# Step groups, statistics and normalisation in an attention and depthwise-convolution kernel

## The chip, the cores and the metric

The kernel runs on one core of a Trainium2 chip, in float32 throughout. The core has a TensorE for matrix products (PE in the profile, with its weight loads as PEld), a VectorE (DVE), a ScalarE (ACT), a GpSimd (POOL) and a SyncE (SP); each works through its own queue in order, and they wait for each other by semaphores. Transfers run on 16 DMA engines; the kernel issues them from SP, from POOL and, at the end, a few from ACT. The metric is the device time of one launch in microseconds (us), as the median of several runs.

## The reference

The input is 16 images of 384 channels and 32 x 32 points. Two residual layers, each behind a group norm over 32 groups of 12 channels:

```
x = x + proj(attention(gn(x)))      # 8 heads of 48, 1024 tokens, softmax over tokens
x = x + dwconv7x7(gn(x), w_sym)     # w_sym: mean of the four rotations of the weight
```

with `gn(v) = (v - mean) / sqrt(var + 1e-5)` per image and group, `attention` from `w_qkv` (3 x 384 rows) with a scale of 48^-0.5, and `proj` with a bias.

## The kernel before, in words

**Layout.** An image is three tiles of 128 channels by 1024 points. The heads are worked in four pairs, called units (u, four an image, 64 in all); the two heads of a pair lie at partitions 0 and 64, so that two products run at once.

**Attention.** A step n is one block of 128 keys against one half of the queries, for a pair: 16 steps a unit, 64 an image, 1024 in all. `s_step` (L331, L339) makes the scores of a step on PE (two products over 48 rows each, into a PSUM tile of two banks) and takes their exponential on ACT into a tile e. `av_step` (L347) multiplies e with v, whose extra column of ones yields the softmax's sum; eight steps accumulate in one PSUM bank, and `take` (L358) copies it out on ACT. The scores' PSUM pool `ps_s` has three buffers, which qk, v, the projection and the convolution on PE use too; `ps_o`, for the sums of AV, has two. The steps go in groups of GS = 4: four S steps, then four AV steps. No maximum is subtracted; the sums are tested at the end (`check_vector`), and a second, general version of the program would run if one were out of range. It doesn't here.

**Around it.** Per image: `qk_step` six times (L280; PSUM copied out on ACT), `v_step` four times (L306, L315), `qk_rest`, which moves the rows of the fourth pair by DMA; after a unit `sums_out`, `invert` and `divide` (through HBM: sums out, reciprocal on DVE, and back broadcast, then a product on DVE, L383); after four units `proj_step` three times (L398), whose ACT copy adds the bias (L406) and whose POOL DMA adds x (L407). The last image ends in a shorter way: `divide_at_once` (L418, L420, L421) sums by a product with a mask and divides at once, `proj_part` (L431) projects with unpacked weights in four parts, and `residual` (L440) adds on DVE.

**Statistics.** `Stats.channels` (L195) takes channel statistics on DVE; `gather` sends them through HBM to one row per group (ch, gs: L201, L203); `groups` (L208 to L220) makes 1/sigma on POOL by a power and sends scale and bias back through HBM (gr, sc). For the first x and the last x1, `groups_on_pe` (L236) does it with small products instead. `apply` normalises: x on ACT (L265), x1 on POOL (L261, three tiles an image) except in the last image.

**Convolution.** For each tile 49 taps on DVE (L455): `scalar_tensor_tensor` adds a shifted, weighted xn to the sum, in place. Up to three tiles are worked in turns, so that neighbouring taps don't depend on each other. Four tiles (two of each of the last two images) are done on PE instead (`conv_on_pe`, L557, 16 pieces, after the attention of the last image), and their result is added on DVE (L570).

**Order.** The order in each queue is written out by a plan while the program is made. It keeps two clocks, `clock` for PE and `vclock` for DVE, advanced by fixed prices (`US_STEP` 1.716 a step, `US_TURN` 0.353 a group, `US_QK` 5.3, `US_V` 4.0, `US_PROJ` 5.3, a tap by its area). `after(wait, cost, f)` puts work for DVE (and the DMAs behind it) on a heap, due `wait` later; `catch_up` issues due work or, if there is none, taps, until `vclock` reaches `clock`. The qk and v work of the next image, `chunks`, is issued between groups as a credit grows. The plan fixes only the order; the true times come from the engines' waits.

Of the kernel before, what the change touches and what calls it, by code (L numbers as in the profile page):

```python
# [16 lines left out]
P = 128  # L17
# [27 lines left out]
def kernel(  # L45
# [64 lines left out]
    def run(general):  # L110
        tag = "g" if general else "f"
        with ExitStack() as stack:
# [11 lines left out]
            epool = pool("epool", 6)  # L124
# [13 lines left out]
            PE_K = [NK - 1, NK - 2]  # L138
            PE_TILES = [(b, k) for b in (B - 2, B - 1) for k in PE_K]

# [24 lines left out]
            nc.sync.dma_start(wp, w_proj_t.rearrange("(k p) c -> p k c", p=P))  # L165
# [7 lines left out]
            vs = []  # L173
            for i in range(2):
                t = wpool.tile([P, NT, VW], F32, name=f"v_{i}")
                nc.gpsimd.memset(t, 1.0)
                vs.append(t)
# [4 lines left out]
            mhalf = wpool.tile([P, NK], F32, name="mhalf")  # L182
            nc.gpsimd.memset(mhalf, -0.5)

# [3 lines left out]
            class Stats:  # L188
# [16 lines left out]
                def groups(self):  # L205

                    mv = small.tile([GROUPS, 2], F32, tag="mv", name=f"mv_{self.name}")
                    nc.vector.bn_aggr(mv, self.gs)  # L208
                    ve = small.tile([GROUPS, 1], F32, tag="ve", name=f"ve_{self.name}")
                    nc.gpsimd.tensor_scalar(ve, mv[:, 1:2], EPS, None, ALU.add)  # L210
                    af = small.tile([GROUPS, 2], F32, tag="af", name=f"af_{self.name}")
                    nc.gpsimd.tensor_tensor(af[:, 0:1], ve, mhalf[0:GROUPS, 0:1], ALU.pow)
                    nc.gpsimd.tensor_tensor(af[:, 1:2], mv[:, 0:1], af[:, 0:1], ALU.mult)
                    nc.gpsimd.tensor_scalar(af[:, 1:2], af[:, 1:2], -1.0, None, ALU.mult)
                    gr_d = ddram.tile([GROUPS, PER, 2], F32, tag="gr", name=f"gr_{self.name}")
                    nc.gpsimd.dma_start(
                        gr_d, af.unsqueeze(1).to_broadcast([GROUPS, PER, 2])
                    )
                    self.sc = small.tile([P, NK, 2], F32, tag="sc", name=f"sc_{self.name}")
                    nc.gpsimd.dma_start(  # L220
                        self.sc, gr_d.rearrange("g e s -> (g e) s").rearrange("(k p) s -> p k s", p=P)
                    )

                def groups_on_pe(self, masks):
# [29 lines left out]
                    nc.gpsimd.tensor_tensor(self.sc[:, :, 0], d, mhalf, ALU.pow)  # L254
# [4 lines left out]
                def apply(self, dst, src, k, engine=None):  # L259
                    if engine is not None:  # L260
                        engine.tensor_scalar(  # L261
                            dst, src, self.sc[:, k, 0:1], self.sc[:, k, 1:2], ALU.mult, ALU.add
                        )
                        return
                    nc.scalar.activation(  # L265
                        dst,
                        src,
                        AF.Identity,
                        bias=self.sc[:, k, 1:2],
                        scale=self.sc[:, k, 0:1],  # L270
                    )

# [28 lines left out]
            def v_step(b, t2):  # L301
# [11 lines left out]
                for j in range(2):  # L313
                    dst = vs[b % 2][:, 2 * t2 + j, 0 : HEADS * (D + 1)]
                    nc.scalar.copy(  # L315
                        dst.rearrange("p (h d) -> p h d", d=D + 1)[:, :, 0:D],
                        ps[:, j, 0:C].rearrange("p (h d) -> p h d", d=D),
                    )

            def v_of(u, i, j):  # L320
                b, p = divmod(u, NP)
                c = (2 * p + j) * (D + 1)
                return vs[b % 2][:, i, c : c + 64]
# [90 lines left out]

            def divide_at_once(u, h):
# [6 lines left out]

            late, pps = {}, {}
# [28 lines left out]
            def conv_tap(b, k, dy, dx):  # L452
                (oy, iy), (ox, ix) = region(dy, dx)
                acc = x1s[b, k].rearrange("p (h w) -> p h w", w=W)[:, oy, ox]
# [199 lines left out]
            clock, vclock = 0.0, 0.0  # L654
# [3 lines left out]
            GS = 4  # L658
            PER_B = 2 * NT * NP

            def now():
                return max(clock, vclock)
# [7 lines left out]
            def us_tap(dy, dx):  # L670
                late_us = 0.06 if active[0][0] >= B - 2 else 0.0
                return ((H - abs(dy)) * (W - abs(dx)) + (130 if len(active) > 1 else 270)) / 940 + late_us

            def tap():
# [3 lines left out]
                if not active:  # L678
                    return 0.0
                b, k, n = active[0]  # L680
                took = us_tap(*TAPS[n])
# [8 lines left out]

            def catch_up(to):
                nonlocal vclock
                while vclock < to:
# [6 lines left out]
                    if took:  # L700
                        vclock += took
                    else:
                        vclock = min([to] + [t[0] for t in later[:1]])

# [21 lines left out]

            def project(b):
# [6 lines left out]
            def x1_part(b, k):  # L734
# [4 lines left out]
                if k == NK - 1:  # L739
                    st.gather()  # L740
                    after(7.0, 0.8, lambda: x1_groups(b, st))

            def x1_groups(b, st):
                st.groups()
                after(9.0, 0.0, lambda: x1_chains(b, st))

            def x1_chains(b, st):
                on_pe = [t for t in PE_TILES if t[0] == b]
                for k in range(NK - 1, -1, -1):
                    tail = b == B - 1  # L750
                    conv_begin(st, b, k, (nc.gpsimd, None, nc.vector)[k] if tail else nc.gpsimd)
# [9 lines left out]
            def begin_x(b):  # L761
                load_x(b)
                after(10.0, 3.8, lambda: x_channels(b))

            def x_channels(b):
# [4 lines left out]
                after(12.0, 0.8, lambda: x_groups(b, st))  # L770

            def x_groups(b, st):
                st.groups()
                after(35.0, 0.0, lambda: x_apply(b, st))

            def x_apply(b, st):
                for k in range(NK):
                    st.apply(xns[b][:, k, :], xns[b][:, k, :], k)
                ready[b] = now() + 6.0

            def finish(u):
                sums_out(u)
                if u < U - 1:
                    after(7.0, 0.3, lambda: finish2(u))
# [5 lines left out]
            def finish3(u):  # L790
                b, p = divmod(u, NP)
                divide(u)
                if p == NP - 1:
                    proj.append((now() + 4.0, b))

            def queue(b):
                chunks.extend(("qk", b, i) for i in range(4))
                chunks.extend(("v", b, i) for i in range(2))
                chunks.extend(("qk", b, i) for i in range(4, 6))
                chunks.extend(("v", b, i) for i in range(2, 4))  # L800
# [5 lines left out]
            st.groups_on_pe(masks_0.rearrange("p (b c) -> p b c", c=P))  # L806
# [5 lines left out]
            while chunks:  # L812
                issue(chunks.popleft())
            vclock = clock
# [41 lines left out]

            credit = 0.0
            for n0 in range(0, NS, GS):
                b, r = divmod(n0, PER_B)
# [5 lines left out]
                for n in range(n0, n0 + GS):  # L865
                    s_step(n)
                if n0 == NS - 2 * GS:
                    after(3.5, 4.2, lambda: None)
                    divide_at_once(U - 1, 0)
                if n0 == NS - GS:  # L870
                    for o in range(NK):
                        proj_part(B - 1, o, (0, 1))
                    clock += 2 * US_PROJ
                for n in range(n0, n0 + GS):
                    av_step(n)
                    u, h, i = n // (2 * NT), n // NT % 2, n % NT
                    if i == NT - 1:
                        take(u, h)
                        if h == 1:
                            finish(u)  # L880
                clock += GS * US_STEP + US_TURN

                credit = min(credit + 12.0 * GS / PER_B, 2.0)
                if proj and proj[0][0] <= clock:
                    project(proj.popleft()[1])
                elif credit >= 2:
                    while chunks and credit >= 1:
                        kind, cb, i = chunks[0]
                        first = {"qk": 2 * NT * (i // 2), "v": 0, "rest": 2 * NT * 3}[kind]
                        if ready.get(cb, 1e9) > clock or r + GS < first:  # L890
                            break
                        issue(chunks.popleft())
                        credit -= 1
                catch_up(clock)
                if b == 1 and r == 0:
                    conv_prepare()
                if b == B - 1:

                    if r == 4 * GS:
# [3 lines left out]
                    if r == 8 * GS:  # L903
                        w4 = w_proj_4.rearrange("(t p) c -> p t c", p=P)
                        nc.sync.dma_start(wp, w4[:, 0:NK])
                        nc.sync.dma_start(late["w3"], w4[:, NK])
                    if r == 6 * GS:
                        conv_matrices(1, flat2(qkpool.tile([P, 2, N], F32, tag="qk", name="mat_1")))
                    if r == 8 * GS:
# [3 lines left out]
                    if r >= 9 * GS and (b, 0) not in x1s and all(c[0] > b - 2 for c in active):  # L913
# [5 lines left out]
                    if r in (10 * GS, 12 * GS, 14 * GS):  # L919
                        loads(1)  # L920


            late["tail"] = True
            b = B - 1
            divide_at_once(U - 1, 1)
            for t in (NP - 2, NP - 1):
                for o in range(NK):
                    proj_part(b, o, (t,))
            clock += US_PROJ * 4 / 3 + 1.0
            st = Stats(f"x1_{b}")  # L930
            for o in range(NK):
                residual(b, o)
                st.channels(x1s[b, o], o)
            conv_piece()
            st.groups_on_pe(late["masks"])
            clock += 7.0
            x1_chains(b, st)
# [58 lines left out]
```

## Time and profile before

| | us |
|---|---|
| median of 3 runs | 3023.71 (3022.39 to 3024.68) |
| the profiled execution, its whole time | 3021.88 |
| its span, first to last instruction | 3020.0 |
| mean granted TensorE clock | 0.994 of full |

Busy time by stage, from the windows of the trace (us busy in the window):

| window | PE | DVE | ACT | POOL |
|---|---|---|---|---|
| 0 to 40 | 22.60 | 8.20 | 4.55 | 9.79 |
| 40 to 260 (first image's attention) | 220.00 | 14.36 | 95.47 | 20.69 |
| 300 to 1000 | 697.78 | 641.51 | 317.19 | 119.57 |
| 1000 to 2000 | 1000.00 | 982.17 | 460.19 | 300.76 |
| 2000 to 2700 | 699.81 | 687.97 | 321.42 | 205.49 |
| 2870 to 2920 (last projection) | 34.64 | 38.28 | 1.83 | 2.76 |
| 2970 to 3020 (end) | 35.48 | 38.46 | 0.00 | 2.13 |

How to read the lines that follow. A line of the chain or of a timeline has its start, its length, the engine, what it does (output <- inputs) and how many instructions it merges; brackets at its end hold the idle time before it and what ended that. A line of a group has the busy time in all and the mean of one in ns, then idle time before it. Matmul ends are modelled, and records of one float32 product come in two.

### The profile page before, as it was taken

To read this page: it belongs to the slowest core of one execution; us is meant where nothing else is said; L and a number is where in the kernel's file an instruction comes from. 1 tells how busy PE (TensorE), PEld (TensorE's weight loads), DVE (VectorE), ACT (ScalarE), POOL (GpSimd) and SP (SyncE) were. 2 spreads that over 40 slices of the span, in tenths; PEclk is the share of its full clock that TensorE was granted. 3 is DMA by queue.
4 is the path that set the end of the run, shared out by engine and by line. 5 is a ranking of instruction groups with operands and counts; after the bars stand their busy time and mean duration, and the time that the engine had idled before them with its cause. 6 is when DMAs were issued, how large, how long until landed. Compare 5 with 4: busy or idle time off the path is not lost.

```text
span 3020.0 us, 30559 instructions
## 1 busy us (share of the span) xinstructions
PE 2970.3 (98%) x11658; PEld 1166.2 (39%) x11658; DVE 2616.1 (87%) x2553; ACT 1298.7 (43%) x1469; POOL 728.3 (24%) x426
## 2 busy tenths in 40 slices
PE   7999999999999999999999999999999999999978
PEld 4333343433334343343434334343433434333333
DVE  1101898997999999999999999999999999999788
ACT  1534535354453545435353453535445353544400
POOL 1021004020140604215060320505133060411500
PEclk9999999999999999999999999999999999999989
DMA  2113031121312112131211313122131312212234
GB/s 70 38 23 67 15 66 37 39 53 33 67 36 58 23 52 51 36 70 39 52 30 36 66 36 66 42 46 37 36 66 36 66 37 51 37 43 38 89 83 114
DMA packets 68332, 149.42 MB, mean 49 GB/s; under 512 B 30880, under 2 KB 33168, under 8 KB 66640
## 3 DMA queue, kind: packets, MB, share of 16 engines
q1 hardware_dynamic: 47536, 90.80, 12.2%
q0 software_dynamic: 18560, 52.31, 7.8%
q10 hardware_dynamic: 2080, 4.26, 0.6%
q8 instruction: 94, 1.54, 0.2%
q14 instruction: 62, 0.51, 0.1%
HBM read 99.35 MB, written 29.49 MB: 43 GB/s over the span
## 4 chain that ended last, share of the span: by engine, by line
PE 90%; DVE 5%; issue 3%; POOL 1%; DMA 1%; ACT 0%; POOLq 0%; SPq 0%; DVEq 0%
PE ps_s L331 29%; PE acc L347 29%; PE ps_qk L280 16%; PE ps_v L306 8%; PE ps_proj L398 8%; DVE x L455 4%; POOL ve_x L210 1%; DMA wc<-in_w_conv 0%; PE ps_st_x L236 0%; DVE bs_x L195 0%; DMA out<-x 0%; DVE x L570 0%; DMA sums<-sum 0%; DMA sum<-o 0%; DVE o L383 0%
## 5 line engine op out<-in xcount | busy, mean ns | idle before, releaser
L455 DVE SCALAR_TENSOR_TENSOR x<-xn,wsym,x 128x960 f32<-128x960 f32 (+9 forms) x2156 | 2379.2, 1175 | 19.5 <-POOL xn L261 17.6
L339 ACT ACTIVATE e<-ps_s 128x1024 f32<-128x1024 f32 x1024 | 967.0, 1030 | 395.0 <-PE ps_s L331 390.1
L331 PE MATMUL ps_s<-qk 48*128 48x512 f32 x4096 | 948.6, 602 | 2.2 <-ACT e L339 2.2
L347 PE MATMUL acc<-e,v 128*64 128x512 f32 x4096 | 935.4, 598 | 0.0
L331 PEld LDWEIGHTS ps_s<-qk 48*128 48x128 f32 x4096 | 373.1, 186 | 566.8 <-issue 430.6
L347 PEld LDWEIGHTS acc<-e,v 128*64 128x64 f32 x4096 | 271.5, 136 | 632.4 <-issue 561.0
L280 PE MATMUL ps_qk<-x,wqk 128*128 128x512 f32 x1152 | 506.8, 596 | 2.3 <-DVE x L261 2.3
L407 POOL DMA_DIRECT2D x<-in_x x45 | 39.6, 881 | 1414.8 <-ACT x L406 1414.8
L280 PEld LDWEIGHTS ps_qk<-x,wqk 128*128 128x128 f32 x1152 | 217.0, 190 | 284.9 <-issue 278.3
L210 POOL TENSOR_SCALAR ve_x<-mv_x 32x1 f32<-32x1 f32 x30 | 313.8, 10461 | 44.4 <-DVE mv_x L208 43.3
L287 ACT COPY qk<-ps_qk 128x1024 f32<-128x1024 f32 x96 | 97.2, 1012 | 463.4 <-PE ps_qk L280 463.4
L306 PE MATMUL ps_v<-wv,x 128*128 128x384 f32 x768 | 254.5, 488 | 0.0
L398 PE MATMUL ps_proj<-o,wp 128*128 128x512 f32 x540 | 235.7, 595 | 0.2 <-DVE bs_x L195 0.2
L358 ACT COPY o<-acc 128x512 f32<-128x512 f32 x128 | 75.1, 587 | 307.2 <-PE acc L347 307.2
L261 POOL TENSOR_SCALAR xn<-x,sc_x 128x1024 f32<-128x1024 f32 x46 | 198.0, 4309 | 33.5 <-DMA sc_x<-gr_x 33.1
L195 DVE BATCH_NORM_STATS2 bs_x<-x 128x6 f32<-128x512 f32 x192 | 120.2, 680 | 98.8 <-DMA x<-in_x 98.7
L306 PEld LDWEIGHTS ps_v<-wv,x 128*128 128x128 f32 x768 | 144.7, 190 | 113.6 <-issue 20.3
L372 DVE RECIPROCAL rec<-sums 128x16 f32<-128x16 f32 x63 | 15.8, 250 | 185.4 <-DMA sums<-sum 185.3
L398 PEld LDWEIGHTS ps_proj<-o,wp 128*128 128x128 f32 x540 | 101.4, 190 | 134.4 <-issue 131.4
L315 ACT COPY v<-ps_v 128x384 f32<-128x384 f32 x128 | 55.1, 483 | 196.9 <-PE ps_v L306 196.9
L406 ACT ACTIVATE x<-ps_proj,bp 128x1024 f32<-128x1024 f32 x45 | 50.1, 1114 | 192.6 <-PE ps_proj L398 175.0
L383 DVE TENSOR_TENSOR o<-o,inv 128x1024 f32<-128x1024 f32 x63 | 76.6, 1216 | 55.5 <-DMA inv<-inv 34.0
(70 smaller groups left out, 486.1 us busy)
## 6 DMA issues: line engine op xcount, KB each, us to landing
inv<-inv SPq DMA_DIRECT2D x126, 256.0 KB
x<-in_x SPq DMA_DIRECT2D x48, 512.0 KB
x<-in_x POOLq DMA_DIRECT2D x48, 512.0 KB, 5.5
out<-x POOLq DMA_DIRECT2D x48, 512.0 KB, 3.5
qk<-qk SPq DMA_DIRECT2D x96, 128.0 KB
sh<-xd SPq DMA_DIRECT2D x38, 160.0 KB
o<-o SPq DMA_DIRECT2D x90, 64.0 KB
sh<-xd ACTq DMA_DIRECT2D x26, 160.0 KB
```

The source lines that it names most:

```text
L195: nc.vector.bn_stats(self.bs[:, k, 6 * h : 6 * h + 6], src[:, h * HALF : (h + 1) * HALF])
L210: nc.gpsimd.tensor_scalar(ve, mv[:, 1:2], EPS, None, ALU.add)
L261: engine.tensor_scalar(dst, src, self.sc[:, k, 0:1], self.sc[:, k, 1:2], ALU.mult, ALU.add)
L280: nc.tensor.matmul(ps[:, h, :], lhsT=wqk[:, k, s, t, :], rhs=xns[b][:, k, h * HALF : (h + 1) * HALF], start=(k == 0), stop=(k == NK - 1),)
L287: nc.scalar.copy(halves(qks[u][:, s, :]), ps)
L306: nc.tensor.matmul(ps[:, j, 0:C], lhsT=xns[b][:, k, t * P : (t + 1) * P], rhs=wv[:, k, :], start=(k == 0), stop=(k == NK - 1),)
L331: nc.tensor.matmul(ps[:, j, :], lhsT=qks[u][r, 1, i * P : (i + 1) * P], rhs=qks[u][r, 0, h * HALF : (h + 1) * HALF], start=True, stop=True,)
L339: nc.scalar.activation(es[n], ps, AF.Exp, scale=SCALE)
L347: nc.tensor.matmul(accs[u, h][64 * j : 64 * j + 64, :], lhsT=v_of(u, i, j), rhs=e[:, j, :], start=(i == 0), stop=(i == NT - 1),)
L383: nc.vector.tensor_tensor(os_[u], os_[u], invs.pop(u), ALU.mult)
L398: nc.tensor.matmul(ps[:, h, :], lhsT=wp[:, t, o * P : (o + 1) * P], rhs=os_[NP * b + t][:, h * HALF : (h + 1) * HALF], start=(t == 0), sto ...
L455: nc.vector.scalar_tensor_tensor(acc, xn1s[b, k].rearrange("p (h w) -> p h w", w=W)[:, iy, ix], wsym[:, k, dy + PAD, dx + PAD : dx + PAD + 1],
```

## The change

- Groups of seven: each image's 64 steps go as eight groups of 7 and one of 8 instead of sixteen of 4. The pool of e grows from 6 to 8. Between the S and the AV half of a group stands a second place for other work (`other`, which issues a projection or chunks of qk, and lets DVE catch up); it is called twice a group.
- v has one buffer, and its four steps are issued in the first group of an image, between S and AV. The load of the next x follows them.
- The first image ends like the last: `divide_at_once`, unpacked projection, `groups_on_pe` (`FAST`, `fast_finish`, `fast_end`). The packed projection weights are loaded in the second image.
- x statistics: images 2 to 15 are streamed through SBUF once in the first image, on POOL's queue, into the x1 buffers; their channel statistics are gathered at once, 1/sigma of all is made, and scale and bias wait in `x_sc`. Image 1 keeps the former way.
- Normalisation: x1 of images 1 to 14 on ACT instead of POOL; x and x1 normalisations are put into ACT's queue after an S half (`applies`), not wherever DVE's plan stood.
- 1/sigma in `groups`: three Newton steps on DVE (`inverse_sigma`) instead of a power on POOL.
- The last image's DVE tile (`LONE`) uses two sums in turns, `sum2` in a buffer of o, added at the end.
- The plan's prices: a tap (area + 128)/955 instead of (area + 130)/940; 0.02 added in the last image instead of 0.06 for the taps of the last two; waits of 9 instead of 7 before `invert`; within `catch_up` the time is `vclock`.

```diff
-            epool = pool("epool", 6)
+            epool = pool("epool", 8)
...
+            FAST = (0, B - 1)
+            LONE = (B - 1, 0)
...
+            def inverse_sigma(dst, mean, var, name):
+                shape = [var.shape[0], var.shape[1]]
+                half = small.tile(shape, F32, tag=f"nh{shape[1]}", name=f"nh_{name}")
+                nc.vector.tensor_scalar(half, var, EPS, 0.5, ALU.add, ALU.mult)
+                y = small.tile(shape, F32, tag=f"ny{shape[1]}", name=f"ny_{name}")
+                nc.vector.tensor_scalar(
+                    y.bitcast(I32), half.bitcast(I32), 1, None, ALU.logical_shift_right
+                )
+                nc.vector.tensor_scalar(
+                    y.bitcast(I32), y.bitcast(I32), -1.0, float(MAGIC), ALU.mult, ALU.add
+                )
+                t = small.tile(shape, F32, tag=f"nt{shape[1]}", name=f"nt_{name}")
+                for _ in range(3):
+                    nc.vector.tensor_tensor(t, y, y, ALU.mult)
+                    nc.vector.tensor_tensor(t, t, half, ALU.mult)
+                    nc.vector.scalar_tensor_tensor(y, t, 1.5, y, ALU.subtract, ALU.mult)
+                nc.vector.tensor_tensor(dst[..., 1], mean, y, ALU.mult)
+                nc.vector.tensor_scalar(dst[..., 0], y, -1.0, None, ALU.mult)
...
-                    nc.gpsimd.tensor_tensor(af[:, 0:1], ve, mhalf[0:GROUPS, 0:1], ALU.pow)
...
+                    inverse_sigma(af.unsqueeze(1), mv[:, 0:1], mv[:, 1:2], self.name)
...
+            def stream_in(b, k):
...
+                many[b, k] = rpool.tile([P, N], F32, tag="x1", name=f"xs_{b}_{k}")
+                nc.gpsimd.dma_start(
+                    many[b, k], x[b, k * P : (k + 1) * P].rearrange("p h w -> p (h w)")
+                )
...
+            def tap_of_two(b, k, c):
...
+                elif n < len(TAPS):
+                    tn = n if n > 1 else 1
+                    conv_tap(b, k, *TAPS[tn], late["sum2"] if n % 2 else None)
+                else:
+                    nc.vector.tensor_tensor(x1s[b, k], x1s[b, k], late["sum2"], ALU.add)
...
             def x1_groups(b, st):
                 st.groups()
-                after(9.0, 0.0, lambda: x1_chains(b, st))
+                applies.append((now() + 10.0, lambda: x1_chains(b, st)))
...
-                    conv_begin(st, b, k, (nc.gpsimd, None, nc.vector)[k] if tail else nc.gpsimd)
+                    conv_begin(st, b, k, (nc.gpsimd, None, nc.vector)[k] if b in (0, B - 1) else None)
...
             def begin_x(b):
                 load_x(b)
-                after(10.0, 3.8, lambda: x_channels(b))
+                if b == 1:
+                    after(10.0, 3.8, lambda: x_channels(b))
+                else:
+                    applies.append((now() + 14.0, lambda: x_apply(b, None)))
...
+            every = [(b, k) for b in range(2, B) for k in range(NK)]
+            for n, bk in enumerate(every):
+                after(4.0 * n, 0.0, lambda bk=bk: stream_in(*bk))
+                after(4.0 * n + 10.0, 1.3, lambda bk=bk: stream_stats(*bk))
+            after(4.0 * len(every) + 14.0, 0.0, stream_gather)
+            after(4.0 * len(every) + 34.0, 3.6, stream_groups)
...
+            def fast_finish(b):
+                nonlocal clock, vclock
+                late["tail"] = b == B - 1
+                proj_part(b, 0, (NP - 2,))
+                divide_at_once(NP * b + NP - 1, 1)
+                for o in range(1, NK):
+                    proj_part(b, o, (NP - 2,))
+                x1_stats[b] = Stats(f"x1_{b}")
+                for o in range(NK):
+                    proj_part(b, o, (NP - 1,))
+                    residual(b, o)
+                    x1_stats[b].channels(x1s[b, o], o)
...
-                for n in range(n0, n0 + GS):
+                for n in range(n0, n0 + size):
                     s_step(n)
...
+                if r == 0 and b - 1 == FAST[0]:
+                    fast_end(b - 1)
+                if r == 0:
+                    for i in range(NT // 2):
+                        issue(("v", b, i))
+                ending = b in FAST and r + size == PER_B
+                if ending:
+                    catch_up(clock)
+                    divide_at_once(NP * b + NP - 1, 0)
+                    vclock += 4.2
                     for o in range(NK):
-                        proj_part(B - 1, o, (0, 1))
+                        proj_part(b, o, (0, 1))
                     clock += 2 * US_PROJ
-                for n in range(n0, n0 + GS):
+                else:
+                    if applies and applies[0][0] <= clock:
+                        applies.popleft()[1]()
+                    other(r + size)
+                for n in range(n0, n0 + size):
                     av_step(n)
```

## The prediction

> **What bounds the kernel now.** I read the page's busy shares first, then the chain that ended last, then the timelines of single engines where the chain is thin.
>
> ```profile
> span 3020.0 us, 30559 instructions
> ...
> PE 2970.3 (98%) x11658; PEld 1166.2 (39%) x11658; DVE 2616.1 (87%) x2553; ACT 1298.7 (43%) x1469; POOL 728.3 (24%) x426
> ```
>
> TensorE (PE) is idle for 49.7 us of 3020.0: 23.7 before its first large matmul, some 15 around the last image's projection, the rest behind its last matmul at 3005.5. So time is won only by giving PE less to do, or by closing those holes. The chain of waits (start, length, what) gives the price of each piece of PE work:
>
> ```profile
> 386.49 7.94 PE ps_v L306 x24
> 394.43 10.30 PE ps_qk L280 x24
> 404.73 7.74 PE ps_v L306 x24
> ...
> 426.90 15.65 PE ps_proj L398 x36
> 442.55 3.63 PE ps_s L331 x16
> ...
> 510.01 10.50 PE ps_qk L280 x24
> ```
>
> The reader is to see that 24 matmul records of one kind cost 10.30 when they follow another full-array product and 10.50 when they follow an attention group. One record is therefore 10.30/24 = 0.429, and a change of kind costs about 0.2. The attention groups, four steps each, further down the chain:
>
> ```profile
> 2760.83 3.63 PE ps_s L331 x16
> 2764.47 3.58 PE acc L347 x16
> 2768.05 3.63 PE ps_s L331 x16
> ```
>
> A step is four records running two by two in S and four in AV (16 records take 3.6, not 6.9), so 4 x 0.429 = 1.717. Four steps are 6.868, yet a group takes 3.63 + 3.585 = 7.217. What is left, 0.35, is the cost of turning from S to AV and back, once a group. The reader is to see that it goes with the number of groups, not of steps.
>
> **What the Trainium skill says.** "TensorEngine Tiling (Array Packing)", Key Properties: changing the tiling mode drains the engine. The trace agrees: S uses 48 rows per product, AV 64 columns, and the weight load that opens a group comes after 0.76 to 0.81 us of idle instead of 0.24. "SBUF — State Buffer", Who interferes with whom: a VectorE (DVE) instruction with two SBUF inputs contends with a GpSimd one that reads SBUF. The trace agrees: the same tap, in a window with the normalisation on GpSimd (1034.5 to 1052) and in one without (1060 to 1200):
>
> ```profile
> L455 DVE SCALAR_TENSOR_TENSOR x<-xn,wsym,x 128x899 f32<-128x899 f32 x6 | 7.3, 1280 | 0.0
> ...
> L455 DVE SCALAR_TENSOR_TENSOR x<-xn,wsym,x 128x899 f32<-128x899 f32 x18 | 19.7, 1141 | 0.0
> ```
>
> **The change part by part**, against the profiled execution of 3021.88 us (span 3020.0 and 1.9 around it), which lies 1.8 below the median of 3023.71.
>
> *Groups of seven.* 64 steps an image make 9 groups instead of 16: 7 x 16 = 112 turns fewer, 112 x 0.35 = **-39.2**. If each of the two changes of kind costs the full 10.50 - 10.30 = 0.20, a turn is 0.40 and the gain 44.8; products that now stand between S and AV give some of it back (below).
>
> *ScalarE (ACT) inside a longer S group.* S writes into three PSUM buffers. ACT's first exponential starts 1.24 after the group's first weight load, and four take 3.77, so one every (3.77 - 1.03)/3 = 0.913; PE makes a step's S in 0.858. PE gains 0.055 a step on ACT, and today's fourth step already touches it:
>
> ```profile
> 1002.79 0.19 PEld L331 LDWEIGHTS ps_s<-qk 48*128 48x128 f32 x2 [0.23 <-issue]
> 1003.28 0.19 PEld L331 LDWEIGHTS ps_s<-qk 48*128 48x128 f32 x2 [0.30 <-ACT e L339]
> 1003.65 0.19 PEld L331 LDWEIGHTS ps_s<-qk 48*128 48x128 f32 x2 [0.18 <-issue]
> ```
>
> The second load is 0.06 late, waiting for ACT, and the third is on time again. Weight loads run ahead, with 0.43 - 0.19 = 0.24 to spare. At the seventh step the delay is 0.06 + 3 x 0.055 = 0.225, still inside; at the eighth 0.28, beyond by 0.04. I take 0.02 for each of 128 groups and 0.1 for each of 16: **+4**. Bounds: 0, and 33 if no delay is absorbed (128 x 0.225 + 16 x 0.28).
>
> *Other products between the groups.* Per image there are four insertions now (two pairs of qk, the v-qk-v block, the projection) and five after (three pairs, v, projection): 0.2 x 15 = **+3**. The 8-buffer pool for e is what seven steps need. One v buffer instead of two costs nothing: its copies (0.86 a pair) follow the products on PE in the order in which AV reads them.
>
> *The first image ends like the last.* Its projection takes four parts instead of three: 48 records in place of 36, that is 12 x 0.429 = 5.2, two sums of 1.06 (L418), and about 1 of waiting for the second reciprocal (3.35 + 0.69 + some 0.4 of hand-over, less the 3.5 of matmuls put over it): +8.5. Then the group averages on PE, 1.72 + 0.65 + 2.71 in the last image now: +5.0. Together **+13.5**. What it buys is on DVE: its chains run without a break from 311.8 now; after, at about 257 (23.7 + qk 30.9 + v 15.6 + attention 113 + next qk 31 + projection 26 + averages and normalisation 16).
>
> *x statistics in the first image.* 42 loads of 512 KB, planned at 4 us each, 84 statistics of 0.65, in a stage where DVE is idle (14.4 of 220 us busy from 40 to 260). The wait is at DMA: large loads stand in front of the small hops of image 1's statistics, and the gathers are 14 times today's. From today's hops (ch 3.2, gs 2.0, gr 4.2, sc 2.8 to landing) they need some 20 and 12 to 30 us against 20 and about 45 available. **+2**, bounds 0 and 40, since ACT, which reads the result, holds the exponentials behind it.
>
> *1/sigma on DVE.* GpSimd's wait (10.5 mean, up to 38) goes, but it is on no PE path. Newton adds 14 small dependent instructions at 0.16 to 0.19 (rows L248 to L252): 2.5 x 15 = 37 on DVE. Moved statistics take 14 x (6 x 0.65 + 0.78) = 65 away, and taps without GpSimd in their way save 2.4 an image (6 x 0.14 + 4 x 0.21 + 3 x 0.26), 34 in all. With the 54 of earlier start DVE stands some 115 better while PE gains about 30. **0** on PE: DVE was only just keeping up and is now ahead. If that cover fails, PE waits at the projection for x1 buffers.
>
> *ScalarE normalises in fixed places.* Three of 1.25 (3.51 together) now lie between the exponentials of one group and the next, twice an image. A group of seven takes 7 x 1.717 + 0.35 = 12.37, ACT needs 1.03 + 6 x 0.913 = 6.51 of it, so 5.86 are free and 2.35 stay over. Queued behind a late normalisation are the next exponentials, and PE after them. The small hops took 8.0 from gr's issue to the normalisation's start (1026.2 to 1034.2); planned are 10, plus up to a group. **0**, bounds below.
>
> *The tail.* PE waits 14.7 at the last projection (start, length, what, and in brackets the idle before it):
>
> ```profile
> 2875.34 1.10 PE L418 MATMUL ps_sum<-o,masks 128*128 128x512 f32 x2 [1.90 <-DVE inv L420]
> 2878.31 8.09 PE L431 MATMUL ps_proj<-o,wp 128*128 128x512 f32 x12 [1.87 <-DVE o L383]
> ...
> 2898.20 7.53 PE L431 MATMUL ps_proj<-o,mat 128*128 128x512 f32 x10 [10.94 <-DVE o L421]
> ```
>
> ```profile
> 2878.18 15.92 DVE L455 SCALAR_TENSOR_TENSOR x<-xn,wsym,x 128x930 f32<-128x930 f32 x13
> 2894.01 3.35 DVE L420 RECIPROCAL inv<-ps_sum 128x512 f32<-128x512 f32 x1
> ```
>
> The reciprocal stood behind 13 taps of older images. With DVE ahead, and matmuls put over the reciprocal, about 2.7 remain: **-12** (bounds 0 and -14.7). Behind it PE has 16 conv pieces of 5.95 and averages, 100 us, unchanged. DVE now ends its taps at 3008.17, 2.7 after PE; with only the last tile's 50 instructions at about 1.13 left it is done well before PE: **-2.5**. The two sums save some 0.1 per tap (1.2 alone, 1.13 in turns), but on DVE, which then has slack: 0.
>
> Sum: -39.2 + 4 + 3 + 13.5 + 2 - 12 - 2.5 = -31.2, so 2990.7 for the profiled execution, 2992.5 as a median.
>
> **Rivals.**
> 1. *The tail stays.* DVE is late against the plan again, and the -12 and -2.5 fail: 3007. For it: the plan's price of a mean tap (917 elements) is cut from (917 + 130)/940 = 1.114 to (917 + 128)/955 = 1.094 and the page gives 2379.2/2156 = 1.104; against: without GpSimd 1.088.
> 2. *ACT sets the S groups.* No delay is absorbed, 33 instead of 4: 3022, no change. Against it: the third load above is on time.
> 3. *Late normalisations (slower).* Place: 29 normalisations in ACT's queue (14 of x1, 15 of x). Point: lateness beyond 2.35 us; each us costs 29, so 1.08 us over it eats the gain, and 2 us over it give 2992.5 + 58 = 3050. For it: hops that go through two DMAs and DVE's order; against: 2 us of spare in the plan.
> 4. *More of it.* Turn 0.40, no delay in S, no gap at either end: -44.8 + 3 + 12.5 - 14.7 - 2.5 = -46.5: 2977.
>
> **How the numbers follow.** Forecast (2980 to 3003) 0.55, tail stays 0.17, ACT-bound 0.08, late normalisations 0.13, more 0.07. This kernel's runs tell about 0.2% (6 us) from no change. Faster: 0.55 + 0.17 + 0.07 and 0.01 of the ACT-bound; same 0.07; slower 0.13. The range runs from case 4's end, 2976, to 3014, above case 1; it leaves out the ACT-bound and the slow case.
>
> **What would show it.** Right: S of seven steps in about 6.2 us and AV in 6.1 with no idle before either; taps of 899 elements near 1141 everywhere; DVE idle for tens of us early on; gaps of under 4 us at the last projection. Wrong: waits of PE on ACT's exponential with ACT waiting on a DMA before it; weight loads late by more than 0.3; a hole at the first image's end; a reciprocal behind taps.

## The result, and the profile after

The changed kernel took 3129.56 us (median of 4 runs, 3126.7 to 3131.81), against 3023.79 before: a ratio of 1.035, 95% interval 1.0332 to 1.0368. The forecast was 2992.5; the time lies outside its range and on the other side. The first lines of the page after (busy time, share of the span, instructions):

```profile
span 3129.7 us, 30693 instructions
...
PE 2972.9 (95%) x11702; PEld 1203.4 (38%) x11702; DVE 2625.8 (84%) x2771; ACT 1327.8 (42%) x1509; POOL 174.9 (6%) x259
```

PE is busy as long as before, 2972.9 against 2970.3, in a span 109.7 longer. Since the turns did go, PE must also run slower somewhere. The list of PE's waits after (who waited for whom, us in total, times, longest) begins:

```profile
PE ps_proj L491 <- DMA o<-o: 124.9, 13, 10.2
PE ps_st_x L266 <- DVE mn_x L275: 13.2, 1, 13.2
```

Before, no wait of PE between its first large product and the last image's projection was longer than 2.2. Now the projections of images 1 to 13 wait 9.6 each for a transfer between two o tiles: the rows of the fourth pair, which `divide` hands to the three others. Image 14's doesn't wait and takes 15.72; in the image after it, the last, no further x is loaded. One image's boundary on PE (start, length, what, idle before it):

```profile
970.23 6.28 PE L424 MATMUL ps_s<-qk 48*128 48x512 f32 x28
976.44 15.75 PE L399 MATMUL ps_v<-wv,x 128*128 128x384 f32 x48
992.12 6.23 PE L440 MATMUL acc<-e,v 128*64 128x512 f32 x28
...
1007.95 18.00 PE L491 MATMUL ps_proj<-o,wp 128*128 128x512 f32 x36 [9.60 <-DMA o<-o]
1025.88 6.28 PE L424 MATMUL ps_s<-qk 48*128 48x512 f32 x28
1032.09 6.23 PE L440 MATMUL acc<-e,v 128*64 128x512 f32 x28
```

The groups are as forecast: from start to start 6.21 for S and 6.16 for AV, together 12.37. The projection comes 9.6 late and then takes 17.9, from start to start, instead of 15.65. Why, SyncE's queue shows at the same place:

```profile
970.96 0.54 SPq L458 DMA_DIRECT2D sum<-o  x2
972.53 0.34 SPq L459 DMA_DIRECT2D sums<-sum  x1
972.93 3.75 SPq L389 DMA_DIRECT2D qk<-qk  x6
992.22 1.31 SPq L152 DMA_DIRECT2D x<-in_x  x3
993.62 0.38 SPq L467 DMA_DIRECT2D inv<-rec  x1
998.77 1.12 SPq L470 DMA_DIRECT2D inv<-inv  x2
1004.81 3.71 SPq L481 DMA_DIRECT2D o<-o  x6
```

The reciprocals of the last unit were made on DVE at 977.51, and the transfer that carries them out (L467) was issued at 993.62. In between nothing was issued but the load of the next x (L152), at 992.22, the moment when PE finished the v products that still read the old x. SyncE works in order: it stood at a load that couldn't start, with the ready transfer behind it. DVE stood too, on the division that needs the result:

```profile
977.51 0.27 DVE L465 RECIPROCAL rec<-sums 128x16 f32<-128x16 f32 x1
...
1003.55 1.23 DVE L476 TENSOR_TENSOR o<-o,inv 128x1024 f32<-128x1024 f32 x1 [16.04 <-DMA inv<-inv]
```

Before, the same queue had these transfers the other way round; 1/sum was out 22 us before the load:

```profile
927.38 0.34 SPq L374 DMA_DIRECT2D inv<-rec  x1
928.80 1.09 SPq L377 DMA_DIRECT2D inv<-inv  x2
949.33 1.29 SPq L150 DMA_DIRECT2D x<-in_x  x3
950.66 4.49 SPq L296 DMA_DIRECT2D qk<-qk  x6
955.25 6.32 SPq L388 DMA_DIRECT2D o<-o  x6
```

The load was a barrier before the change too: PE finished v at 949.2 and the load went out at 949.33, and the rows, whose division on DVE had ended at 945.0, came behind it at 955.25. It did no harm, because the projection was not due until 963.7.

The slowed projection has its own reason. Windows of the trace after (PE, PEld, DVE, ACT, POOL busy, then granted clock, DMA share, GB/s): the wait, the projection's first 4.1 us, and a later part of it.

```profile
998.30:1007.90 9.60, 0.05 (x2) 0.00 (x0) 4.35 (x4) 0.00 (x0) 0.00 (x0) 0.71 0.34 76
1007.90:1012.00 4.10, 4.05 (x5) 1.83 (x6) 4.10 (x5) 0.00 (x0) 0.00 (x0) 0.50 0.29 47
1012.00:1016.00 4.00, 4.00 (x10) 1.74 (x9) 4.00 (x4) 0.32 (x1) 0.00 (x0) 0.92 0.00 0
```

PE starts again at half clock and is back at the full one after 4 to 5 us. The Trainium skill says so ("TensorE: Matmul & The Clock Gate", Part 1: an idle window of about 3.4 us puts the array to half rate, a busy one back); the trace agrees, 0.50 after 9.6 idle. Further down, in b1 and a2, shorter waits, from 2.1 us on, led to it as well; there the measurement counts. So an image loses 9.6 + 2.3, and 13 images some 155 us, more than the whole difference: without it 3129.6 - 155 = 2975.

### The profile page after: what moved, and what is told of

Read it like the earlier page. It is cut to its first block, busy times and chain, and to the rows that moved or that the text cites. A ratio compares the mean times of both kernels' runs of the same rounds, so it can differ in the third digit from the quotient of the medians.

```text
span 3129.7 us, 30693 instructions
## 1 busy us (share of the span) xinstructions
PE 2972.9 (95%) x11702; PEld 1203.4 (38%) x11702; DVE 2625.8 (84%) x2771; ACT 1327.8 (42%) x1509; POOL 174.9 (6%) x259
## 4 chain that ended last, share of the span: by engine, by line
PE 85%; issue 8%; DMA 4%; DVE 2%; SPq 1%; POOL 0%; ACT 0%; DVEq 0%; POOLq 0%
PE ps_s L424 27%; PE acc L440 25%; PE ps_qk L373 16%; PE ps_proj L491 8%; PE ps_v L399 7%; DMA inv<-rec 1%; PE ps_conv L650 1%; DMA inv<-inv 1%; DMA o<-o 1%; PE ps_proj L523 1%; DVE x L548 1%; DVE o L476 1%; PE ps_st_x L266 0%; SPq L152 0%; SPq L481 0%
## 5 line engine op out<-in xcount | busy, mean ns | idle before, releaser
L548 DVE SCALAR_TENSOR_TENSOR x<-xn,wsym,x 128x960 f32<-128x960 f32 (+9 forms) x2132 | 2330.3, 1173 | 18.0 <-ACT xn L295 16.5
L432 ACT ACTIVATE e<-ps_s 128x1024 f32<-128x1024 f32 x1024 | 954.5, 1045 | 243.5 <-PE ps_s L424 239.5
L424 PE MATMUL ps_s<-qk 48*128 48x512 f32 x4096 | 918.2, 596 | 0.0
L440 PE MATMUL acc<-e,v 128*64 128x512 f32 x4096 | 910.7, 596 | 0.0
L440 PEld LDWEIGHTS acc<-e,v 128*64 128x64 f32 x4096 | 281.2, 137 | 608.4 <-issue 599.8
L491 PE MATMUL ps_proj<-o,wp 128*128 128x512 f32 x504 | 250.0, 660 | 124.9 <-DMA o<-o 124.9
L451 ACT COPY o<-acc 128x512 f32<-128x512 f32 x128 | 76.3, 596 | 344.3 <-PE acc L440 344.3
L229 DVE BATCH_NORM_STATS2 bs_x<-x 128x6 f32<-128x512 f32 x108 | 69.2, 686 | 61.7 <-DMA x<-in_x 61.5
L650 PE MATMUL ps_conv<-sh,mat 128*32 128x496 f32 (+3 forms) x896 | 96.1, 587 | 2.1 <-DMA sh<-xd 2.1
L318 DVE BATCH_NORM_STATS2 bs_all<-xs 128x6 f32<-128x512 f32 x84 | 52.2, 678 | 23.7 <-DMA xs<-in_x 23.7
L295 ACT ACTIVATE xn<-x,sc_x 128x1024 f32<-128x1024 f32 x44 | 52.1, 1283 | 26.8 <-DVE sc_x L285 26.8
```

The costliest lines, as they stand in the source:

```text
L229: nc.vector.bn_stats(self.bs[:, k, 6 * h : 6 * h + 6], src[:, h * HALF : (h + 1) * HALF])
L424: nc.tensor.matmul(ps[:, j, :], lhsT=qks[u][r, 1, i * P : (i + 1) * P], rhs=qks[u][r, 0, h * HALF : (h + 1) * HALF], start=True, stop=True,)
L432: nc.scalar.activation(es[n], ps, AF.Exp, scale=SCALE)
L440: nc.tensor.matmul(accs[u, h][64 * j : 64 * j + 64, :], lhsT=v_of(u, i, j), rhs=e[:, j, :], start=(i == 0), stop=(i == NT - 1),)
L451: nc.scalar.copy(os_[u][:, h * HALF : (h + 1) * HALF], accs.pop((u, h)))
L491: nc.tensor.matmul(ps[:, h, :], lhsT=wp[:, t, o * P : (o + 1) * P], rhs=os_[NP * b + t][:, h * HALF : (h + 1) * HALF], start=(t == 0), sto ...
```

## The experiments

Theory Q is that the order in SyncE's queue makes the loss. Its rivals: P, the plan sets the projection too early whatever the queue does; C, the lower clock is the cause and not a result of the waits; and, without a letter, the DMA bandwidth that the x load takes from the small transfers beside it.

**a1**: the load goes behind the two hops of 1/sum and the rows, by putting it on the plan's heap.

```diff
                     if i == NT // 2 - 1 and b + 1 < B:
-                        begin_x(b + 1)
+                        after(0.0, 0.0, lambda: begin_x(b + 1))
```

> The changed kernel with one line moved: the load of the next x is put on the plan's heap instead of being issued with the last v step, so that in SyncE's queue the two transfers of 1/sum and the six of the fourth pair's rows stand before it. Theory Q (SyncE's order: the 1/sum of the last unit stands behind an x load that waits for the v products): the 13 waits of 9.6 us before the projection go to under 1 us each, the projection falls from 18.0 to 15.7, and the time is 3130 - 13 x (9.6 + 2.3) = 2975. Rival P (the plan sets the projection too early, whatever the queue does): waits stay near 9 us and the time near 3130. Rival C (TensorE's granted clock of 0.975 is the cause): the clock stays below 0.98 and the projection at 18.

Measured: 2973.7 us, 0.9833 of the kernel before (0.9816 to 0.9849). The projection's waits are gone, it takes 15.72, the mean clock is 0.997. PE and SyncE's queue at the same boundary:

```profile
939.74 15.75 PE L399 MATMUL ps_v<-wv,x 128*128 128x384 f32 x48
955.42 6.23 PE L440 MATMUL acc<-e,v 128*64 128x512 f32 x28
961.58 15.72 PE L491 MATMUL ps_proj<-o,wp 128*128 128x512 f32 x36
```

```profile
941.02 0.35 SPq L467 DMA_DIRECT2D inv<-rec  x1
943.93 1.12 SPq L470 DMA_DIRECT2D inv<-inv  x2
951.89 3.69 SPq L481 DMA_DIRECT2D o<-o  x6
955.68 1.48 SPq L152 DMA_DIRECT2D x<-in_x  x3
```

The load now goes out at 955.68, which is 0.3 after PE has finished v (955.42): it lost nothing. Q gives the number: 2975 was expected, and one place in one queue is the whole loss.

**a2, a3, a4** come at the same wait from three sides: a2 sends 1/sum through GpSimd's queue, a3 the x load through GpSimd's, and a4 puts the projection later.

```diff
# a2
-                nc.sync.dma_start(inv_d.rearrange("j (p c) -> (j p) c", c=SC), rec)
+                nc.gpsimd.dma_start(inv_d.rearrange("j (p c) -> (j p) c", c=SC), rec)
...
# a3
-                    nc.sync.dma_start(
+                    (nc.gpsimd if b > 1 else nc.sync).dma_start(
                         xns[b][:, k, :], x[b, k * P : (k + 1) * P].rearrange("p h w -> p (h w)")
...
# a4
-                    proj.append((now() + 4.0, b))
+                    proj.append((now() + 16.0, b))
```

> The changed kernel with the three transfers of 1/sum (out and back) issued from GpSimd's queue instead of SyncE's; the x load stays where it is, and the six small row transfers still stand behind it in SyncE's queue. Theory Q: 1/sum is back some 15 us earlier, but the rows go out only after the x load's issue at the end of the v products, so 2 to 5 us of the 9.6 stay before the projection: 3010 to 3050. Rival P: near 3130. If bandwidth taken by the x load is what matters and not the queue, no more than the 3.7 us that the small transfer was slowed by are won: about 3080.

Measured: 3025.54 us, ratio 1.0004 (0.9996 to 1.0013). The waits fall from 124.9 to 38.2, 13 times again. The rows still stood behind the load, as expected, and most projections start at reduced clock:

```profile
976.43 17.39 PE L491 MATMUL ps_proj<-o,wp 128*128 128x512 f32 x36 [3.48 <-DMA o<-o]
```

> The changed kernel with the x loads of images 2 to 15 issued from GpSimd's queue; SyncE's order is otherwise unchanged. Theory Q: SyncE never waits for the v products, 1/sum and rows go out when they are ready, the waits before the projection fall under 1 us, 2970 to 2985. Rival P: near 3130. A new wait is possible on GpSimd, whose queue then waits for the v products with the x1 additions and stores behind it; it would show as ScalarE or VectorE waiting for these, and cost up to 5 us an image.

Measured: 2983.93, ratio 0.9868 (0.9851 to 0.9884). Of the 13 waits one is left, 4.9, in the first of these images; SyncE is free of the load. The feared wait through GpSimd's queue shows only as one of 2.3 for a normalisation. These two waits and the slow projection after the first (18.66 instead of 15.72) make up the 10 us between a3 and a1. a1 moved the due time of x's normalisation in the plan along with the load; a3 leaves that alone, so it isn't what made the waits.

> The changed kernel with the projection's due time 16 us after the division in the plan instead of 4; queues unchanged. Theory Q: the division still comes 16 us late, and VectorE still idles for it, but TensorE has a group of steps to do meanwhile: waits before the projection near 0, 2972 to 2990. Rival C: clock and time as in the changed kernel. If instead the lateness only moves on with the projection, the waits stay.

Measured: 2981.76, ratio 0.9861 (0.9844 to 0.9877). P is right in this: the projection can step aside, and PE then doesn't feel the wait. DVE still does; its list of waits has 71.4 us on 1/sum's transfer. P and Q are two ends of one thing: the transfer became late by the queue, and the plan had no slack for it. That a1, which changes no due time of the projection, loses nothing shows that the queue made the lateness. What leaves a4 8 us above a1 was not taken apart.

**a5** splits the lateness: the queue still stands in the old place, at a load of 32 columns, and the rest of x comes later.

```diff
+                        load_head(b + 1)
-                        begin_x(b + 1)
+                        after(0.0, 0.0, lambda: begin_x(b + 1))
...
             def begin_x(b):
-                load_x(b)
+                load_rest(b)
```

> Splits the lateness of 1/sum into its two parts. The first 32 of 1024 columns of each x tile are loaded in the old place in SyncE's queue (three small transfers, which wait for the v products as the whole load did); the rest is put behind the rows of the fourth pair, as in a1. So the queue still stands, but no large load is in flight beside the small transfers. If the standing queue alone made the wait: 9.6 us less the 3.7 that the small transfer lost and about 1 to 2 of the next two, 4 to 5 us before each projection and a slowed restart, 13 x (4.5 + 1.7) over 2974: about 3055. If the bandwidth taken by the x load made it: no waits, about 2975.

Measured: 3084.8, ratio 1.0197 (1.018 to 1.0214). Waits of 76.3 us, 13 times, 5.9 each. PE, and SyncE's queue ahead of it:

```profile
992.98 18.28 PE L508 MATMUL ps_proj<-o,wp 128*128 128x512 f32 x36 [5.80 <-DMA o<-o]
```

```profile
981.05 1.31 SPq L154 DMA_DIRECT2D x<-in_x  x3
982.45 0.38 SPq L484 DMA_DIRECT2D inv<-rec  x1
983.95 1.12 SPq L487 DMA_DIRECT2D inv<-inv  x2
```

So the standing queue alone makes 5.9 of the 9.6, and the 1.5 MB of x in flight beside the small transfers the other 3.7. The queue shows where: from the issue of the 8 KB of 1/sum to the next step it takes 1.50 here and 5.15 in the changed kernel. The time is 30 above what I expected: the waits are 1.4 longer than my 4.5, and a restart costs 2.6 where I had put 1.7. 13 x (5.9 + 2.6) = 110 over a1's 2974 is 3084.

The next three are made on a1, to price the other terms of the forecast's sum.

**b1**, groups of four again:

```diff
-            SIZES = [7] * 8 + [8]
+            SIZES = [4] * 16
...
-                credit = min(credit + 0.45, 2.0)
+                credit = min(credit + 0.25, 2.0)
...
-                if b == B - 1 and r in (35, 42, 49):
+                if b == B - 1 and r in (36, 44, 52):
```

> a1 with groups of four steps (16 an image instead of 9; the credit for other work scaled with the number of groups). Prices the turn alone: 112 turns of 0.35 are 39, so 3013; with 0.40 a turn 3019. If long groups cost something that short ones don't (ScalarE behind in S), less than 39: below 3010.

Measured: 3041.75, ratio 1.0054 (1.0038 to 1.0071), 68 above a1 where I expected 39. Two projections in a row in its timeline:

```profile
978.61 15.69 PE L491 MATMUL ps_proj<-o,wp 128*128 128x512 f32 x36 [2.12 <-DMA o<-o]
1158.72 15.69 PE L491 MATMUL ps_proj<-o,wp 128*128 128x512 f32 x36 [1.75 <-DMA o<-o]
```

An image takes 180.11, of which 1.75 is waiting; 178.36 less a1's 175.84 is 2.5, or 7 turns of 0.36. The price of a turn holds. The list of waits has 22.1 more, 12 times, at the projection, since shorter groups bring it nearer to the division. And three of its projections, after waits of 2.10, 3.05 and 2.27, ran at reduced clock (17.39, 18.60 and 17.29 instead of 15.69), which is 6 more. 39 + 22 + 6 are 67 of the 68.

**b2**, the first image ended like the middle ones:

```diff
-            FAST = (0, B - 1)
+            FAST = (B - 1,)
...
-                nc.sync.dma_start(wp, w4[:, 0:NK])
-                late["w3"] = npool.tile([P, N], F32, tag="xn1", name="w3_0")[:, 0:C]
-                nc.sync.dma_start(late["w3"], w4[:, NK])
+                nc.sync.dma_start(wp, w_packed)
...
-                    conv_begin(st, b, k, (nc.gpsimd, None, nc.vector)[k] if b in (0, B - 1) else None)
+                    conv_begin(st, b, k, (nc.gpsimd, None, nc.vector)[k] if b == B - 1 else None)
...
-                    nc.sync.dma_start(wp, w_packed)
```

> a1 with the first image ended like the middle ones (1/sum through memory, packed projection with a DMA addition, statistics through memory) and only the last one in the short way. TensorE then has 12 records less in the first projection, no two sums and no averages: about 12 us less work, 2962, if VectorE can do without its earlier start. Rival: VectorE loses some 50 us of tap time at the start, stays behind the plan to the end, and gives 10 to 15 us back in the last projection or at x1 buffers: 2972 or more.

Measured: 2959.05, ratio 0.9785 (0.9768 to 0.9801), and 2958.01 with the same ratio (0.9772 to 0.9797) when run once more:

> The same kernel as b2 (a1 with the first image ended like the middle ones), timed beside the next one: 2957 to 2961 again.

It is 15 below a1. The short ending of the first image costs PE what the forecast said (13.5) and buys nothing that PE feels: DVE's taps run from 307 instead of 255, and the last projection still has no gap.

**b3**, x1 normalised on GpSimd again:

```diff
-                    conv_begin(st, b, k, (nc.gpsimd, None, nc.vector)[k] if b in (0, B - 1) else None)
+                    conv_begin(st, b, k, (nc.gpsimd, None, nc.vector)[k] if b in (0, B - 1) else nc.gpsimd)
```

> a1 with the normalisation of x1 of images 1 to 14 back on GpSimd, at the place that the change gave it in the plan. Taps beside it slow by 0.14 to 0.26 us, some 34 us of VectorE time in all, as in the kernel before. If TensorE alone sets the end: 2974 within 3. If VectorE is at its limit too: up to 34 more, about 3000, with waits at the last projection.

Measured: 2982.54, ratio 0.9863 (0.9847 to 0.9879), 9 above a1, between the two expectations. Slowed taps are not the reason: those of 899 elements take 1143 ns in the mean, as in a1 (1145). Where this kernel normalises, DVE is out of taps and waits for GpSimd, and the last projection has a gap again (first DVE's waits, then PE's); that the first makes the second is argued, not shown:

```profile
DVE x L548 <- POOL xn L291: 39.6, 12, 3.3
...
PE ps_proj L523 <- DVE o L515: 5.2, 1, 5.2
```

Statistics of x image by image, as before, were not tried on the changed kernel, so what that part of the change is worth stays open.

**c2 and c3** look for a faster version, from b2: groups of eight.

```diff
-            SIZES = [7] * 8 + [8]
+            SIZES = [8] * 8
...
-                if b == B - 1 and r in (35, 42, 49):
+                if b == B - 1 and r in (32, 40, 48):
```

> b2 with eight groups of 8 steps an image instead of eight of 7 and one of 8. One turn of 0.35 less for each of 16 images is 5.6 us: 2953. If the eighth S step is held by ScalarE (my estimate was 0.04 to 0.1 a group beyond the seventh), 128 groups take 5 to 12 back: 2958 to 2965.

Measured: 2962.31, ratio 0.9801 (0.9788 to 0.9814), not below b2. But an image takes 175.50 against b2's 175.85, the turn saved and no more; the loss is one wait, in image 1. ACT and PE there, and GpSimd's queue:

```profile
304.37 3.50 ACT L293 ACTIVATE xn<-x,sc_x 128x1024 f32<-128x1024 f32 x3 [10.41 <-DMA sc_x<-gr_x]
```

```profile
309.32 6.77 PE L422 MATMUL ps_s<-qk 48*128 48x512 f32 x20 [7.09 <-ACT e L430]
```

```profile
274.32 8.81 POOL L584 DMA_DIRECT2D wsh<-w_d  x16 [9.52 <-DMA w_d<-wsym]
...
288.87 0.81 POOL L233 DMA_DIRECT2D ch_x<-bs_x  x1 [0.23 <-issue]
```

DVE had x1's statistics ready at 275; their transfer stood behind the small ones that prepare the convolution on PE, until 288.87. ACT reached the normalisation and waited 10.4, its exponentials behind it, and PE 7.1. This is the forecast's third rival, once.

```diff
-                if b == 1 and r == 0:
+                if b == 1 and r == 32:
                     conv_prepare()
```

> c2 with the preparation of the convolution on TensorE (24 small transfers on GpSimd's queue, 9 us waiting for one of them and 15 us of issuing) moved from the first group of image 1 to the middle of that image. In c2 the statistics of the first x1 stood behind it, ScalarE waited 10.4 us for them with its exponentials behind, and TensorE 7.1. If that one wait is why groups of 8 did not gain over b2: it vanishes, with its restart, and the time is 2962 - 7.1 - 2 = 2953. If the eighth step itself costs: still 2960 or more.

Measured: 2951.84 us, ratio 0.976 (0.9747 to 0.9774), the fastest of all and 5.7% below the changed kernel. PE has no wait left in the loop; what stays is the start (12.5 and 2.3) and under 3 in all at the averages and the convolution.

## Why the prediction was wrong

**The step that failed** is the sentence "One v buffer instead of two costs nothing". It looked at the copies on ACT and the order on PE. With one buffer the v products move from the middle of an image to its first group, and the load of the next x, which waits for them, moves too, past the hops of the last unit's 1/sum in SyncE's queue. The forecast listed the new place of v and counted its turn, and did not count the load that is issued with it, nor look at what stands behind a load that has to wait. Its price was 13 x (9.6 + 2.3) = 155; a1 takes it away, and nothing else of the change, and gives 2973.7.

**The rest of the sum** forecast 2990.7 for the profiled execution, and a1's is 2973.8, 17 less. By its terms:
- Turns, -39.2: right. S and AV take 12.37 a group of seven, an image 175.84 where the sum implies 178.1 - 2.45 + 0.2 = 175.85, and b1 gives 0.36 a turn.
- ACT in a longer S group, +4: it was 0. Neither the seventh nor the eighth step waits (6.21; 7.07 = 8 x 0.858 + 0.2).
- The first image's ending, +13.5: near, by b2 (15). The +2 for late transfers there: no such wait of PE shows.
- The tail, -12: it was larger. In a1 the last projection has no gap at all:

```profile
2849.76 1.02 PE L512 MATMUL ps_sum<-o,masks 128*128 128x512 f32 x2
2850.62 3.60 PE L523 MATMUL ps_proj<-o,wp 128*128 128x512 f32 x8
2854.06 5.52 PE L523 MATMUL ps_proj<-o,mat 128*128 128x512 f32 x12
```

That is -14.7. The restarts go as well, which the forecast left out though they stood in the lines it showed: 12 records took 8.09 after the gap and ten 7.53, where 0.43 each would be 5.2 and 4.3, so 6 us of reduced clock (the granted clock is 0.50 there). With PE's first large product at 22.16 instead of 23.69, the terms 4 + 2 + 2.7 + 6.1 + 1.5 make 16 of the 17. Since the first image's ending cost 1 to 2 more than its term, 2 to 3 us have no place.

One reading of the page was off, and no term rests on it: of the 23.7 us before the first large product PE is idle for 17.4 and busy for 6.3 with the averages of the first x.

**The rivals.** The slower one had a 0.13 chance and named late normalisations on ACT. That mechanism exists (c2, 7.1 us), but not in the changed kernel, where PE never waits for ACT. So the side was thought of, and its place was wrong: it is a queue that issues DMAs, not a compute engine. The ACT-bound rival fell with the S groups, and the tail did not stay.

**DVE** was rightly held to be off the path: in a1 PE waits for it only at the start and at the averages. What the 34 us of taps slowed by GpSimd were worth, b3 doesn't tell, since its taps were not slowed.

## What to carry to other kernels

When work is moved, list the DMAs that hang on it and what stands behind each in its queue; a load that waits for a buffer is a barrier for every ready transfer behind it, and it costs nothing to put it behind those, as long as its buffer isn't free earlier. After such a wait add the restart: PE loses more than the idle time that the profile shows. And read a change's parts one by one: here a misplaced load (155 us) hid a gain of 50, of which one part (the first image's short ending) was itself a loss of 15.

## What the runs showed of the hardware

- What PE loses to reduced clock after a wait isn't proportional to the wait. After 9.2 to 10.2 us of idle (the changed kernel) the projection takes 17.7 to 18.5, after 5.6 to 6.1 (a5) 18.1 to 18.8, after 4.9 (a3) 18.7, against 15.7 without a wait: 2 to 3 us lost. Below that it goes both ways: 15.69 after waits of 1.1 to 1.9, 2.12 and 2.23 (b1) and of 2.63 and 2.91 (a2), but about 17.4 after 2.10 and 2.27 (b1) and after ten of 2.6 to 3.5 (a2), and 18.6 after 3.05 (b1). What decides between 2.1 and 2.9 us, no run here shows.
- A transfer of 8 KB took 5.15 us from issue to the next step with 1.5 MB of loads issued just ahead of it (993.62 to 998.77 in the changed kernel), and 1.50 in the same place without them (982.45 to 983.95 in a5). Behind the six small row transfers of qk it took 2.91 (941.02 to 943.93 in a1).
- S with three PSUM buffers ran eight steps without a wait in c3, though an exponential comes every 0.92 us (eight take 7.44, one 1.03) and a step on PE every 0.858.
